# Graph attention on one Trainium2 core: the value product turned, and score rows made on TensorE instead of by DMA

## The chip, the cores and the metric

The kernel runs on one core of one Trainium2 chip. The core has TensorE (PE: matmuls and transposes, with PEld its weight loads), VectorE (DVE), ScalarE (ACT), GpSimd (POOL) and SyncE (SP, which here only issues DMAs). Matmul results land in PSUM, [...]; everything else lives in SBUF or in DRAM. The metric is the device time of one execution in microseconds, less is better. The kernel before takes 3081.6 us, the median of three runs (3081.55 to 3082.2).

## The reference

64 graphs of 256 nodes with 256 features, and an adjacency matrix each. Layer 0 is a normalised, rectified input through three rounds of a gated graph network (message product, sum over neighbours, GRU cell), added to the input. Layer 1 is graph attention with four heads of 64 features, added again:

```python
h = (node_feats @ W.T + b).reshape(Bb, Nn, Hh, Cc)
l_src = jnp.einsum('bihc,hc->bih', h, a_src)
l_dst = jnp.einsum('bjhc,hc->bjh', h, a_dst)
logits = jax.nn.leaky_relu(l_src[:, :, None, :] + l_dst[:, None, :, :], ALPHA)
logits = jnp.where(adj_matrix[..., None] == 1, logits, NEG_INF)
probs = jax.nn.softmax(logits, axis=2)
out = jnp.einsum('bijh,bjhc->bihc', probs, h)
```

For a node i and a head, the score of neighbour j is a number of i plus a number of j; the softmax over j weighs the value vectors h of all j. All of it is f32.

## The kernel before, in words

The graphs are worked on in 32 pairs. A pair is T = 512 nodes: PB = 2 graphs of KN = 2 tiles of 128 nodes, R = 4 tiles r. `pair(p)` is a Python generator that writes out the work of one pair and yields between steps. The loop at the end keeps two pairs alive and takes one step of each in turn: pair p is in the second half of its steps (end of the GRU, then attention) while pair p+1 is in its first half (normalisation, GRU). A pair has 23 yields (`STEPS`), and a new pair starts every `STEPS // 2 + 1` = 12 steps. The order in which steps are written gives each instruction a priority; a planner in the framework then makes one instruction stream per engine, in which work of a later step goes ahead where an earlier one would leave the engine idle by the planner's own costs. On the chip each engine takes its stream in order, and waits on semaphores that the framework places.

PSUM is split in two pools of four banks: `ps_g` for the GRU gates, and `ps_m`, tag `mm`, handed out by `bank(...)`, for every other TensorE result. A bank is free again when its readers are done.

The steps of a pair: normalise and transpose (L242 to L247); three rounds of halves / aggregate / two gate steps (L248 to L303, `gate` at L233); `x1`, the sum with the input (L306); normalise again (L314); `val` (L316), for each tile of nodes 264 columns: 256 value features, then 4 numbers of i and 4 of j, one per head. Then come the steps that the change touches:

- Score rows (L326 to L335). The four j-columns of `val` are transposed into a [4, 512] block `prow` (4 transposes), copied to SBUF as `srow` by ScalarE, written to DRAM (`flat`) and read back onto all 128 partitions as `rows_` by a second DMA, both on SP's queue.
- Scores (L338 to L350), one step per graph: for each tile of 128 nodes i and each head, VectorE adds row, i-number and mask into `zz` [128, 4, 256], then applies the leaky slope in place.
- Softmax (L351 to L374), one step per tile: negated maximum on VectorE, exponentials on ScalarE with their sum `den`, reciprocal `rden`, and 8 transposes (`ppT`), whose copies, one by each of ScalarE and VectorE, make `prT`: probabilities with j on the partitions.
- Value product (L375 to L387), at the start of the next step: for each head and each half of j, `prT` is stationary (128 columns) and 64 value columns are moving; the result `po` has i on the partitions. VectorE multiplies by `rden` into `o`, GpSimd adds `x1`, and after both graphs SP stores `o`.

Of the kernel before, what the change touches and what calls it, by code (L numbers as in the profile page):

```python
# [9 lines left out]
F32 = mybir.dt.float32  # L10
# [3 lines left out]
ALU = mybir.AluOpType  # L14
AX = mybir.AxisListType

P = 128
# [3 lines left out]
ALPHA = 0.2  # L21
# [4 lines left out]
def gated_gnn_then_gat_kernel(  # L26
# [27 lines left out]
    nc = tc.nc  # L54
    B, N, D = x.shape
    L = weight.shape[0]
    H, C2 = a.shape
    C = C2 // 2
    G = 3 * D // P
    KD = D // P  # L60
    KN = N // P
    PB = 2
    R = PB * KN
    T = PB * N
# [3 lines left out]
    ctx.enter_context(nc.allow_non_contiguous_dma(reason="biases and attention vectors, once"))  # L68
    const = ctx.enter_context(tc.tile_pool(name="const", bufs=1))
    io = ctx.enter_context(tc.tile_pool(name="io", bufs=2))  # L70
    dram = ctx.enter_context(tc.tile_pool(name="dram", bufs=2, space=bass.MemoryType.DRAM))
    ps_g = ctx.enter_context(tc.tile_pool(name="ps_g", bufs=4, space=bass.MemoryType.PSUM))
    ps_m = ctx.enter_context(tc.tile_pool(name="ps_m", bufs=4, space=bass.MemoryType.PSUM))

    def bank(name):
        return ps_m.tile([P, 512], F32, tag="mm", name=name)
# [23 lines left out]
    ident = const.tile([P, P], F32, name="ident")  # L100
# [138 lines left out]
    def pair(p):  # L239
# [82 lines left out]
                )  # L322
            nc.vector.tensor_add(val[:, r, :], pt[:, :VW], b_val)
        yield

        pt = bank(f"prow_{p}")  # L326
        for r in range(R):
            nc.tensor.transpose(pt[:H, ts(r, P)], val[:, r, D + H :], ident)
        srow = small.tile([H, T], F32, tag="srow", name=f"srow_{p}", bufs=2)
        nc.scalar.copy(srow, pt[:H, :])  # L330
        flat = dram.tile([H, T], F32, tag="flat", name=f"flat_{p}")
        nc.sync.dma_start(flat, srow)
        rows_ = sb.tile([P, H, T], F32, tag="rows", name=f"rows_{p}")
        nc.sync.dma_start(rows_, bass.AP(tensor=flat.tensor, offset=flat.offset, ap=[[0, P], [T, H], [1, T]]))
        yield  # L335
        o = sb.tile([P, R, D], F32, tag="o", name=f"o_{p}")
        for i in range(PB):
            lks = []  # L338
            for s in range(KN):
                r = i * KN + s  # L340
                zz = sb.tile([P, H, N], F32, tag="zz", name=f"zz_{p}_{r}")
                for h in range(H):
                    nc.vector.scalar_tensor_tensor(  # L343
                        zz[:, h, :], rows_[:, h, ts(i, N)], val[:, r, D + h : D + h + 1],
                        noedge[:, r, :], op0=ALU.add, op1=ALU.add,
                    )
                zf = zz.rearrange("q h n -> q (h n)")
                nc.vector.scalar_tensor_tensor(zf, zf, ALPHA, zf, op0=ALU.mult, op1=ALU.max)
                lks.append(zz)
            yield  # L350
            for s in range(KN):  # L351
                r = i * KN + s
                lk = lks[s]
                nmx = small.tile([P, H], F32, tag="nmx", name=f"nmx_{p}_{r}")
                nc.vector.tensor_reduce(nmx, lk, AX.X, ALU.max, negate=True)  # L355
                den = small.tile([P, H], F32, tag="den", name=f"den_{p}_{r}")
                pr = sb.tile([P, H, N], F32, tag="pr", name=f"pr_{p}_{r}")
                for h in range(H):
                    nc.scalar.activation(  # L359
                        pr[:, h, :], lk[:, h, :], AF.Exp, bias=nmx[:, h : h + 1], accum_out=den[:, h : h + 1]  # L360
                    )
                rden = small.tile([P, H], F32, tag="rden", name=f"rden_{p}_{r}")
                nc.vector.reciprocal(rden, den)
                prT = sb.tile([P, KN, H, P], F32, tag="prT", name=f"prT_{p}_{r}")
                for j in range(KN):
                    pt = bank(f"ppT_{p}_{r}_{j}")
                    for h in range(H):
                        nc.tensor.transpose(pt[:, ts(h, P)], pr[:, h, ts(j, P)], ident)  # L368
                    dst = prT[:, j].rearrange("q h n -> q (h n)")
                    if j % 2:  # L370
                        nc.vector.tensor_copy(dst, pt)
                    else:
                        nc.scalar.copy(dst, pt)  # L373
                yield  # L374
                po = bank(f"po_{p}_{r}")  # L375
                for h in range(H):
                    for j in range(KN):
                        nc.tensor.matmul(  # L378
                            po[:, ts(h, C)], prT[:, j, h, :], val[:, i * KN + j, ts(h, C)],
                            start=(j == 0), stop=(j == KN - 1),  # L380
                        )
                nc.vector.tensor_mul(  # L382
                    o[:, r, :].rearrange("q (h c) -> q h c", h=H),
                    po[:, :D].rearrange("q (h c) -> q h c", h=H),
                    rden[:, :, None].to_broadcast([P, H, C]),
                )
                nc.gpsimd.tensor_add(o[:, r, :], o[:, r, :], x1[:, r, :])  # L387
        nc.sync.dma_start(out_rows[ts(p, T), :].rearrange("(r q) d -> q r d", q=P), o)


    STEPS = 1 + L * (2 + KD) + 4 + PB * (1 + KN)
    live = []
    nxt, tick = 0, 0
    while nxt < NPAIR or live:
# [38 lines left out]
```

## Time and profile before

| | before |
|---|---|
| median of the runs | 3081.6 us |
| the profiled execution, its span | 3082.2 us, 3080.4 us |
| granted TensorE clock, mean | 0.986 |
| TensorE busy (matmul) | 2895.8 us, 94% |
| VectorE, ScalarE, GpSimd busy | 56%, 33%, 18% |
| DMA, mean | 29 GB/s |
| value product `po`, L378 | 2048 instructions |
| probability transposes `ppT`, L368 | 1024 instructions |
| read-back `rows<-flat` | 32 DMAs of 1024 KB |

How to read it: an engine's busy share is an average over the span. Matmuls are pipelined, so the durations of single ones overlap, and their sum overstates the work; the distance between the starts of a long run of the same kind is the cost of one. In a row of groups, the operands are out<-in, then partitions x elements, the count, busy time, mean ns of one, and the idle time of the engine just before them with what ended it.

### The profile page before, as it was taken

To read this page: it belongs to the slowest core of one execution; us is meant where nothing else is said; L and a number is where in the kernel's file an instruction comes from. 1 tells how busy PE (TensorE), PEld (TensorE's weight loads), DVE (VectorE), ACT (ScalarE), POOL (GpSimd) and SP (SyncE) were. 2 spreads that over 40 slices of the span, in tenths; PEclk is the share of its full clock that TensorE was granted. 3 is DMA by queue.
4 is the path that set the end of the run, shared out by engine and by line. 5 is a ranking of instruction groups with operands and counts; after the bars stand their busy time and mean duration, and the time that the engine had idled before them with its cause. 6 is when DMAs were issued, how large, how long until landed. Compare 5 with 4: busy or idle time off the path is not lost.

```text
span 3080.4 us, 30164 instructions
## 1 busy us (share of the span) xinstructions
PE 2895.8 (94%) x11236; PEld 1668.7 (54%) x11236; DVE 1715.3 (56%) x3390; ACT 1021.9 (33%) x2247; POOL 559.0 (18%) x583
## 2 busy tenths in 40 slices
PE   7999999999999999999999999999999999999995
PEld 4455555555555555555555555555555555555554
DVE  3465655555664556554556554656555555645554
ACT  1233333333332333332333333333323333323332
POOL 0121111112112121111211111111111112111111
PEclk9999999999999999999999999999999999999996
DMA  2000000000001001001000100000010010000000
GB/s 84 21 21 28 28 34 29 21 29 33 28 28 35 21 28 35 28 28 35 21 28 29 34 28 33 23 28 28 28 35 21 28 35 28 28 35 8 21 21 21
DMA packets 60947, 88.84 MB, mean 29 GB/s; under 512 B 4736, under 2 KB 56576, under 8 KB 56704
## 3 DMA queue, kind: packets, MB, share of 16 engines
q1 hardware_dynamic: 55552, 84.16, 8.0%
q10 hardware_dynamic: 5248, 2.76, 0.3%
q8 instruction: 88, 1.44, 0.2%
q14 instruction: 59, 0.48, 0.1%
HBM read 69.87 MB, written 17.04 MB: 28 GB/s over the span
## 4 chain that ended last, share of the span: by engine, by line
PE 83%; DVE 9%; ACT 3%; POOL 3%; issue 1%; DMA 1%; SPq 0%; DVEq 0%; POOLq 0%; ACTq 0%
PE pr L235 19%; PE pz L235 19%; PE pin L235 11%; PE phn L235 8%; PE po L378 8%; PE pa L264 7%; PE pv L320 4%; PE ppT L368 3%; ACT pr L359 2%; PE pn L228 2%; POOL d L299 1%; DVE x L310 1%; DVE st_b L199 1%; DVE zz L343 1%; DVE nmx L355 1%
## 5 line engine op out<-in xcount | busy, mean ns | idle before, releaser
L289 POOL TENSOR_SCALAR z<-z 128x512 f32<-128x512 f32 x192 | 140.5, 732 | 1310.9 <-ACT z L288 1310.9
L235 PE MATMUL pr<-aggr,w_in 128*128 128x512 f32 x768 | 361.0, 592 | 0.0
L235 PE MATMUL pz<-aggr,w_in 128*128 128x512 f32 x768 | 360.9, 592 | 0.0
L235 PE MATMUL pin<-aggr,w_in 128*128 128x512 f32 x768 | 360.9, 592 | 0.0
L285 ACT ACTIVATE r<-pr,brz 128x512 f32<-128x512 f32 x192 | 131.9, 687 | 688.6 <-PE pr L235 688.6
L294 DVE TENSOR_TENSOR t<-pin,t 128x512 f32<-128x512 f32 x192 | 132.5, 690 | 359.6 <-PE pin L235 358.5
L300 DVE TENSOR_TENSOR d<-z,d 128x512 f32<-128x512 f32 x192 | 132.9, 692 | 328.9 <-POOL d L299 327.9
L359 ACT ACTIVATE pr<-zz,nmx 128x256 f32<-128x256 f32 x512 | 254.3, 500 | 105.6 <-DVE nmx L355 105.6
L378 PEld LDWEIGHTS po<-val,prT 128*128 128x128 f32 x2048 | 253.1, 196 | 41.2 <-issue 14.8
L288 ACT ACTIVATE z<-pz,brz 128x512 f32<-128x512 f32 x192 | 131.3, 684 | 397.0 <-PE pz L235 397.0
L286 DVE TENSOR_SCALAR r<-r 128x512 f32<-128x512 f32 x192 | 81.6, 425 | 323.0 <-ACT r L285 323.0
L378 PE MATMUL po<-val,prT 128*128 128x64 f32 x2048 | 256.5, 277 | 2.4 <-ACT prT L373 1.6
L235 PE MATMUL phn<-hT,hh_T 128*128 128x512 f32 x512 | 254.8, 599 | 0.0
L235 PE MATMUL pr<-hT,hh_T 128*128 128x512 f32 x512 | 252.8, 596 | 0.0
L235 PE MATMUL pz<-hT,hh_T 128*128 128x512 f32 x512 | 246.0, 592 | 0.0
L235 PEld LDWEIGHTS pin<-aggr,w_in 128*128 128x128 f32 x768 | 145.9, 190 | 183.7 <-issue 183.7
L235 PEld LDWEIGHTS pz<-aggr,w_in 128*128 128x128 f32 x768 | 145.9, 190 | 183.7 <-issue 183.7
L235 PEld LDWEIGHTS pr<-aggr,w_in 128*128 128x128 f32 x768 | 143.5, 190 | 156.0 <-issue 146.1
L387 POOL TENSOR_TENSOR o<-o,x 128x256 f32<-128x256 f32 x128 | 107.0, 836 | 648.8 <-DVE o L382 609.2
L343 DVE SCALAR_TENSOR_TENSOR zz<-rows,val,noedge 128x256 f32<-128x256 f32 x512 | 214.8, 476 | 7.2 <-DMA rows<-flat 7.2
L368 PE MATMUL ppT<-ident,pr 128*128 128x128 f32 x1024 | 164.5, 285 | 49.8 <-ACT pr L359 44.8
L299 POOL TENSOR_TENSOR d<-hT,n 128x512 f32<-128x512 f32 x128 | 161.6, 1263 | 188.0 <-ACT n L296 188.0
(96 smaller groups left out, 4343.2 us busy)
## 6 DMA issues: line engine op xcount, KB each, us to landing
rows<-flat SPq DMA_DIRECT2D x32, 1024.0 KB
x<-in_x_dram SPq DMA_DIRECT2D x32, 512.0 KB
adj<-in_adj_dram SPq DMA_DIRECT2D x32, 512.0 KB
out_dram<-o SPq DMA_DIRECT2D x32, 512.0 KB
w_msg<-in_L_gnn_weight_dram ACTq DMA_DIRECT2D x1, 768.0 KB
ih_nat<-in_L_gnn_w_ih_dram ACTq DMA_DIRECT2D x1, 768.0 KB
hh_nat<-in_L_gnn_w_hh_dram ACTq DMA_DIRECT2D x1, 768.0 KB
flat<-srow SPq DMA_DIRECT2D x32, 8.0 KB
```

What stands on the lines that cost most here:

```text
L235: nc.tensor.matmul(pt, w[:, k, ts(g, P)], src[:, k, :], start=start and k == 0, stop=stop and k == KD - 1)
L264: nc.tensor.matmul(pt[:, ts(i, N)], y[:, r, ts(e, P)], edge[:, r, :], start=(j == 0), stop=(j == len(parts) - 1),)
L285: nc.scalar.activation(r_, p_r, AF.Tanh, bias=brz[:, g_r : g_r + 1], scale=0.5)
L288: nc.scalar.activation(z_, p_z, AF.Tanh, bias=brz[:, g_z : g_z + 1], scale=0.5)
L289: nc.gpsimd.tensor_scalar(z_, z_, 0.5, 0.5, op0=ALU.mult, op1=ALU.add)
L294: nc.vector.tensor_add(t_, p_in, t_)
L299: nc.gpsimd.tensor_sub(d_, hT[:, c, :], n__)
L300: nc.vector.tensor_mul(d_, z_, d_)
L343: nc.vector.scalar_tensor_tensor(zz[:, h, :], rows_[:, h, ts(i, N)], val[:, r, D + h : D + h + 1], noedge[:, r, :], op0=ALU.add, op1=ALU.add,)
L359: nc.scalar.activation(pr[:, h, :], lk[:, h, :], AF.Exp, bias=nmx[:, h : h + 1], accum_out=den[:, h : h + 1])
L368: nc.tensor.transpose(pt[:, ts(h, P)], pr[:, h, ts(j, P)], ident)
L378: nc.tensor.matmul(po[:, ts(h, C)], prT[:, j, h, :], val[:, i * KN + j, ts(h, C)], start=(j == 0), stop=(j == KN - 1),)
```

## The change

Two parts of attention are replaced, and the steps are cut differently.

The score rows no longer go through DRAM. For each graph, head and half of j, TensorE transposes one column of `val`, broadcast to 128 columns, so that every partition of the result holds the row: 8 transposes per graph into two banks `rowp`, each with two heads. VectorE reads them from PSUM, and the leaky slope now writes a second tile `lk`.

The value product is turned. `prT` collects both tiles of a graph, so that a head's probabilities are [128 of j, 256 of i] and are moving, and the 64 value columns of the head are stationary. The result has features on the partitions: head 2 h2 on 0 to 63 and head 2 h2 + 1 on 64 to 127 of one bank `po`. ScalarE copies it to `oT`, four transposes per graph turn it back into a bank `pob`, and one multiply and one add per graph (512 columns, not 256) finish it. The product now waits for both tiles of the graph, and the transposes back stand one step later.

`STEPS` becomes 24: the step for the rows is gone, and each graph has one more for the turning back. The interval between pairs becomes 13.

```diff
-        pt = bank(f"prow_{p}")
-        for r in range(R):
-            nc.tensor.transpose(pt[:H, ts(r, P)], val[:, r, D + H :], ident)
-        srow = small.tile([H, T], F32, tag="srow", name=f"srow_{p}", bufs=2)
-        nc.scalar.copy(srow, pt[:H, :])
-        flat = dram.tile([H, T], F32, tag="flat", name=f"flat_{p}")
-        nc.sync.dma_start(flat, srow)
-        rows_ = sb.tile([P, H, T], F32, tag="rows", name=f"rows_{p}")
-        nc.sync.dma_start(rows_, bass.AP(tensor=flat.tensor, offset=flat.offset, ap=[[0, P], [T, H], [1, T]]))
-        yield
         o = sb.tile([P, R, D], F32, tag="o", name=f"o_{p}")
         for i in range(PB):
+            rowp = []
+            for h2 in range(H // 2):
+                pt = bank(f"prow_{p}_{i}_{h2}")
+                for hh in range(2):
+                    col = D + H + 2 * h2 + hh
+                    for s in range(KN):
+                        nc.tensor.transpose(
+                            pt[:, hh * N + s * P : hh * N + (s + 1) * P],
+                            val[:, i * KN + s, col : col + 1].to_broadcast([P, P]),
+                            ident,
+                        )
+                rowp.append(pt)
...
                     nc.vector.scalar_tensor_tensor(
-                        zz[:, h, :], rows_[:, h, ts(i, N)], val[:, r, D + h : D + h + 1],
+                        zz[:, h, :], rowp[h // 2][:, ts(h % 2, N)], val[:, r, D + h : D + h + 1],
                         noedge[:, r, :], op0=ALU.add, op1=ALU.add,
                     )
-                zf = zz.rearrange("q h n -> q (h n)")
-                nc.vector.scalar_tensor_tensor(zf, zf, ALPHA, zf, op0=ALU.mult, op1=ALU.max)
-                lks.append(zz)
+                lk = sb.tile([P, H, N], F32, tag="lk", name=f"lk_{p}_{r}")
+                zf, lf = (y.rearrange("q h n -> q (h n)") for y in (zz, lk))
+                nc.vector.scalar_tensor_tensor(lf, zf, ALPHA, zf, op0=ALU.mult, op1=ALU.max)
+                lks.append(lk)
             yield
+            prT = sb.tile([P, KN, H, N], F32, tag="prT", name=f"prT_{p}_{i}")
+            rden = small.tile([P, KN, H], F32, tag="rden", name=f"rden_{p}_{i}")
...
-                    dst = prT[:, j].rearrange("q h n -> q (h n)")
+                    dst = prT[:, j, :, ts(s, P)]
+                    src = pt.rearrange("q (h n) -> q h n", h=H)
...
                 yield
-                po = bank(f"po_{p}_{r}")
-                for h in range(H):
-                    for j in range(KN):
+            po = bank(f"po_{p}_{i}")
+            for h2 in range(H // 2):
+                for j in range(KN):
+                    for hh in range(2):
+                        h = 2 * h2 + hh
                         nc.tensor.matmul(
-                            po[:, ts(h, C)], prT[:, j, h, :], val[:, i * KN + j, ts(h, C)],
+                            po[hh * C : (hh + 1) * C, ts(h2, N)], val[:, i * KN + j, ts(h, C)], prT[:, j, h, :],
                             start=(j == 0), stop=(j == KN - 1),
                         )
-                nc.vector.tensor_mul(
-                    o[:, r, :].rearrange("q (h c) -> q h c", h=H),
-                    po[:, :D].rearrange("q (h c) -> q h c", h=H),
-                    rden[:, :, None].to_broadcast([P, H, C]),
-                )
-                nc.gpsimd.tensor_add(o[:, r, :], o[:, r, :], x1[:, r, :])
+            oT = sb.tile([P, H // 2, N], F32, tag="oT", name=f"oT_{p}_{i}")
+            nc.scalar.copy(oT.rearrange("q h n -> q (h n)"), po)
+            yield
+            pb_ = bank(f"pob_{p}_{i}")
+            for s in range(KN):
+                for h2 in range(H // 2):
+                    nc.tensor.transpose(pb_[:, s * D + h2 * P : s * D + (h2 + 1) * P], oT[:, h2, ts(s, P)], ident)
+            rows = slice(i * KN, (i + 1) * KN)
+            nc.vector.tensor_mul(
+                o[:, rows, :].rearrange("q r (h c) -> q (r h) c", h=H),
+                pb_.rearrange("q (x c) -> q x c", c=C),
+                rden.rearrange("q s h -> q (s h)")[:, :, None].to_broadcast([P, KN * H, C]),
+            )
+            of, xf = (y[:, rows, :].rearrange("q r d -> q (r d)") for y in (o, x1))
+            nc.gpsimd.tensor_add(of, of, xf)
...
-    STEPS = 1 + L * (2 + KD) + 4 + PB * (1 + KN)
+    STEPS = 1 + L * (2 + KD) + 3 + PB * (2 + KN)
```

More of the change, by code (lines that the diff above doesn't have):

```diff
@@ L70, in gated_gnn_then_gat_kernel @@
     io = ctx.enter_context(tc.tile_pool(name="io", bufs=2))
-    dram = ctx.enter_context(tc.tile_pool(name="dram", bufs=2, space=bass.MemoryType.DRAM))
     ps_g = ctx.enter_context(tc.tile_pool(name="ps_g", bufs=4, space=bass.MemoryType.PSUM))
@@ L361, in pair @@
                     )
-                rden = small.tile([P, H], F32, tag="rden", name=f"rden_{p}_{r}")
-                nc.vector.reciprocal(rden, den)
-                prT = sb.tile([P, KN, H, P], F32, tag="prT", name=f"prT_{p}_{r}")
+                nc.vector.reciprocal(rden[:, s, :], den)
                 for j in range(KN):
@@ L368, in pair @@
                         nc.tensor.transpose(pt[:, ts(h, P)], pr[:, h, ts(j, P)], ident)
-                    dst = prT[:, j].rearrange("q h n -> q (h n)")
+                    dst = prT[:, j, :, ts(s, P)]
+                    src = pt.rearrange("q (h n) -> q h n", h=H)
                     if j % 2:
-                        nc.vector.tensor_copy(dst, pt)
+                        nc.vector.tensor_copy(dst, src)
                     else:
-                        nc.scalar.copy(dst, pt)
+                        nc.scalar.copy(dst, src)
```

## The prediction

> **What bounds the kernel now.** I read the page first: busy time by engine and the chain that ended last.
>
> ```profile
> span 3080.4 us, 30164 instructions
> PE 2895.8 (94%) x11236; PEld 1668.7 (54%) x11236; DVE 1715.3 (56%) x3390; ACT 1021.9 (33%) x2247; POOL 559.0 (18%) x583
> ...
> PE 83%; DVE 9%; ACT 3%; POOL 3%; issue 1%; DMA 1%; SPq 0%; DVEq 0%; POOLq 0%; ACTq 0%
> ```
>
> TensorE is busy 94% of the span and holds 83% of the chain; no other engine passes 56%. Work taken off or put on TensorE should therefore move the end, and work on the others should not, unless TensorE comes to wait for it. The waits of TensorE itself are the second view (total us, times, longest):
>
> ```profile
> PE pt_b L219 <- DVE xn_b L206: 78.7, 32, 4.4
> PE ppT L368 <- ACT pr L359: 44.8, 33, 13.1
> PE pn_b L228 <- DVE hT L301: 24.1, 32, 4.2
> ```
>
> Each comes about once per pair. None is for the score rows. The only wait for those is VectorE's, in the groups:
>
> ```profile
> L343 DVE SCALAR_TENSOR_TENSOR zz<-rows,val,noedge 128x256 f32<-128x256 f32 x512 | 214.8, 476 | 7.2 <-DMA rows<-flat 7.2
> ```
>
> It is 7.2 us in all, in the last pair. The transfer is hidden everywhere else.
>
> Busy durations of matmuls overlap, so I price TensorE from the third view, the timeline, by start to start:
>
> ```profile
> 1295.76 1.89 PE L378 MATMUL po<-val,prT 128*128 128x64 f32 x16
> 1297.49 1.94 PE L235 MATMUL phn<-hT,hh_T 128*128 128x512 f32 x4
> 1299.26 1.88 PE L235 MATMUL pr<-hT,hh_T 128*128 128x512 f32 x4
> 1300.98 1.88 PE L235 MATMUL pr<-aggr,w_in 128*128 128x512 f32 x4
> ...
> 1307.84 1.04 PE L368 MATMUL ppT<-ident,pr 128*128 128x128 f32 x8
> 1308.72 0.38 PE L228 MATMUL pn<-ident,hT 128*128 128x128 f32 x2
> 1309.12 0.43 PE L378 MATMUL po<-val,prT 128*128 128x64 f32 x2
> ...
> 1350.43 3.73 PE L320 MATMUL pv<-w_val,hT_b 128*128 128x264 f32 x16
> 1353.99 1.88 PE L235 MATMUL pr<-aggr,w_in 128*128 128x512 f32 x4
> ```
>
> One `po` instruction takes (1297.49 - 1295.76)/16 = 0.108 us, a gate instruction of 512 columns 1.72/4 = 0.43, a transpose 0.88/8 = 0.11, a 264-column one 3.56/16 = 0.2225. An f32 product is two instructions (the 1024 products of L378 are 2048), a transpose one. `po` moves 64 columns, an eighth of a gate's, yet costs a quarter of a gate's time: it pays for loading 128 weight columns, not for streaming. The same place of the pattern (`po` x2) starts at 1309.12 and again at 1401.92, so a pair takes 92.8 us. TensorE's own work per pair: gates 144 x 0.43 = 61.9; `pa` 48 x 0.119 = 5.7 (16 instructions take 1.9); the transposes `pn`, `pt`, `prow`, `ppT` 76 x 0.11 = 8.4; `pv` 3.6; `po` 64 x 0.108 = 6.9. That is 86.5, which leaves 6.3 us per pair of waits and ramps.
>
> [...] a gate matmul lasts 592 ns, 0.43 of which is its turn, so its tail is about 0.16 us. [...]
>
> **The change, part by part**, per pair of graphs unless said.
>
> *Score rows.* Removed: 4 `prow` transposes (0.44), one ScalarE copy (575 ns), two DMAs on SP's queue. Added: 16 transposes of one column broadcast to 128, at 0.11 as the other 128x128 ones: 1.76. Net +1.32 on TensorE. A broadcast operand is not in the trace; loading 4 columns (`prow`) and 128 columns both gave 0.11, because the streamed identity sets the pace, so below 0.11 I see nothing and the upper bound is the 0.19 of an f32 weight load (+1.3); I take 0.11. SP loses waits for `srow` and issues x, adj and out no later; VectorE waited only 10.6 us for x in the whole span, so that is worth nothing. VectorE's zz now reads PSUM. From L343 (476 ns, 256 elements) and L348 (1218, 1024) a 512-element one is 723 ns in SBUF, and L291 from PSUM takes 750: 27 ns x 512 = 14 us of VectorE in the span, hidden by its 44% of idle time.
>
> *The product.* Removed: 64 `po` instructions, 6.91. Added: 8 products per graph, 16 instructions of 256 columns. A turn is 0.43/2 = 0.215 (0.2225 x 256/264 = 0.216 agrees). In order of issue each head's two instructions follow each other, then the other head's two: the second of one head can run beside the first of the other. So 16 instructions make 9 turns, 1.94 us a graph, 3.87 a pair. Entirely serial it is 6.88.
>
> *Turning back.* 8 transposes: 0.88. ScalarE gains a 512-column copy (586 ns, x64, less `srow`: +19 us in the span), VectorE does 64 multiplies of 690 instead of 128 of 423, GpSimd 64 adds of 1263 instead of 128 of 836: all off the path. The transposes wait for that copy, and gates queue behind them on TensorE; but they stand a step later, behind the other pair's `pa` or gates, which cover 0.6 us. Uncovered it would be 0.59 + 0.16 = 0.75 a graph.
>
> *Mode switches.* In before one `po` block in four is split by a gate (the x2 at 1309.12). I take 2.5 blocks per pair, 5 switches x 0.163 = 0.82. Lower bound 0; upper, with the next weight load exposed too, 5 x (0.163 + 0.19) = 1.77.
>
> *Steps.* 23 becomes 24 and a new pair starts every 13 steps, not 12: the last gate step of the third round has no partner step. Neighbouring work is planned ahead across steps (the next pair's `st_a` runs at 1532), so nothing on TensorE is lost. The zz step moves from beside `halves` to beside gates (10.3 us), which may end the 0.94 us wait of `ppT`; in exchange the later product has less to put into the wait for `hT`. I count them as even.
>
> *Banks.* Two of the four `mm` banks are held while VectorE does zz, 8 x 0.42 (214.8 us of L343 over 512) + 1.22 = 4.6 us at least. Gates, which run beside it, use the other pool, so I cost it at nothing; without this cover it is up to 4.6 x 64 us.
>
> Sum: 3.87 + 1.76 + 0.88 + 0.82 - 7.35 = -0.02 a pair, **-1 us** over 32 pairs.
>
> *The end.* The last pair's attention runs alone. There zz starts at 3041.97, when the rows land, while the first two tiles of `val` stand at 3033.0 and `pv` ends at about 3034. Eight cold transposes (0.22) put the start near 3036: -6. Two `po` blocks of 3.7 become one of 9 x 0.43 = 3.9 per graph, -3; copy, transposes and the longer multiply and add cost +2 to +3 at the very end. **-7 us**.
>
> So 3082.2 (the profiled execution; its span is 3080.4, 1.8 around it) - 8 = 3074.2; the median of the runs is 0.6 lower: **3074**.
>
> **The rivals.**
>
> *A, heads side by side (the forecast), 60%.* Its own range: without switch costs -0.84 x 32 = -27, and -10 at the end: 3045; with the dear switches +0.93 x 32 = +30, -7: 3104.
>
> *B, the two heads run one after the other, 30%; this is the one on the other side.* Place: the product; 6.88 in place of 3.87 and no gain over the 6.91 removed, so all 16 + 8 - 4 transposes are net cost: +2.17 x 32 = +69, less 5 at the end: **3146**, between 3116 (the `ppT` wait of 30 us filled) and 3172 (switches too). For it: no trace shows f32 column tiles, and each pass reloads weights. [...] It decides from 7.35 - 2.64 = 4.71 us a pair: a factor of 6.88/4.71 = 1.46 between the heads breaks even, 1.77 with the five switches.
>
> *C, side by side, but a wait takes the place, 10%.* TensorE stands at the transposes back until the ScalarE copy is done, or at a `mm` bank: 64 x 0.75 = 48 us: **3122**. For it: in-order issue, four banks. Against: ScalarE is busy 33%.
>
> *The row transfer was on the path and its removal is the gain.* Only 7.2 us of waiting speaks for it; that is inside the -7.
>
> **How the numbers follow.** A repeat of this kernel can tell 0.2% (6 us). A: faster in 0.55 of it, same 0.2, slower 0.25; B and C are slower. Faster 0.33, same 0.12, slower 0.55. A is likeliest, hence 3074, with its own range 3045 to 3104. The whole range goes up into B, to 3155: left out are about a tenth of A and the upper third of B, under 2 in 10.
>
> **What would show it.** Right: two products of different heads start within some ns of each other, 16 of them in about 2 us, then a gap near 0.16 before the next kind; the DMA share falls; the waits of TensorE keep their three lines. Wrong: 16 products in 3.4 us (B); a new line of TensorE waiting for `oT` or for zz (C); broadcast transposes over 0.11 apart; gaps over 0.3 at each switch.

## The result, and the profile after

The changed kernel takes 3149.9 us, the median of four runs (3145.84 to 3150.82), against 3081.68 us of the kernel before in the same series: a ratio of 1.0219, with a 95% interval from 1.0201 to 1.0236. It is 68 us slower. The forecast was 3074 us. The profiled execution took 3145.84 us with a span of 3144.0, where before it was 3082.2 and 3080.4.

The page of the kernel after: its span, the busy time by engine, and the chain that ended last.

```profile
span 3144.0 us, 29237 instructions
...
PE 2948.7 (94%) x10852; PEld 1599.2 (51%) x10852; DVE 1708.7 (54%) x3326; ACT 1031.8 (33%) x2279; POOL 538.9 (17%) x519
...
PE 77%; DVE 9%; POOL 6%; issue 4%; ACT 3%; DMA 1%; SPq 0%; DVEq 0%; POOLq 0%; ACTq 0%
```

TensorE issues 384 instructions fewer and shows 53 us more of busy time. Its share of the chain falls from 83% to 77%, and what gains is GpSimd (3 to 6%) and issue (1 to 4%). The waits of TensorE after (total us, times, longest):

```profile
PE pt_b L218 <- DVE xn_b L205: 78.6, 32, 4.3
PE pn L227 <- DVE hT L300: 25.1, 64, 1.7
PE pv L319 <- ACT hT_b L219: 18.2, 32, 0.6
PE ppT L371 <- ACT pr L364: 12.8, 6, 6.0
```

Against before, the wait of `ppT` fell from 44.8 to 12.8 us; two came in its place. One is `pn` for hT, which stood so among the waits before:

```profile
PE pn L228 <- DVE hT L301: 3.3, 2, 1.7
```

The other is `pv` for `hT_b` (0.5 us, once, before). Together these waits changed by 32 us down and 40 up, so waits alone don't explain 68 us. The groups of the kernel after that answer to the score rows and the product, by line (busy us, mean ns of one, then idle time before and what ended it):

```profile
L385 PE MATMUL po<-prT,val 128*64 128x256 f32 x1024 | 180.7, 401 | 2.4 <-ACT prT L377 0.9
L319 PE MATMUL pv<-w_val,hT_b 128*128 128x264 f32 x512 | 172.1, 506 | 18.2 <-ACT hT_b L219 18.2
L395 PE MATMUL pob<-ident,oT 128*128 128x128 f32 x256 | 38.4, 272 | 1.4 <-ACT oT L390 1.4
L344 DVE SCALAR_TENSOR_TENSOR zz<-prow,val,noedge 128x256 f32<-128x256 f32 x512 | 211.8, 476 | 59.4 <-PE prow L333 59.4
```

The surprise is the second row. The value projection `pv`, which the change does not touch, is 506 ns an instruction now. Before, its row was:

```profile
L320 PE MATMUL pv<-w_val,hT_b 128*128 128x264 f32 x512 | 123.2, 395 | 0.5 <-ACT hT_b L220 0.5
```

The last row of the groups after shows VectorE waiting 59.4 us for the rows, where it waited 7.2 us for the DMA before.

Two stretches of the timeline (start us, duration, then the instructions) show where TensorE's time goes. First the end of a GRU round of one pair beside the value product of the other:

```profile
1308.34 0.38 PE L227 MATMUL pn<-ident,hT 128*128 128x128 f32 x2
1308.74 0.65 PE L385 MATMUL po<-prT,val 128*64 128x256 f32 x4
1309.32 1.13 PE L234 MATMUL phn<-hT,hh_T 128*128 128x512 f32 x2
1310.38 1.51 PE L385 MATMUL po<-prT,val 128*64 128x256 f32 x10
1312.58 0.87 PE L227 MATMUL pn<-ident,hT 128*128 128x128 f32 x6 [0.69 <-DVE hT L300]
1313.38 0.65 PE L385 MATMUL po<-prT,val 128*64 128x256 f32 x2
1313.96 1.12 PE L234 MATMUL phn<-hT,hh_T 128*128 128x512 f32 x2
```

The heads do run side by side: four `po` instructions take 1309.32 - 1308.74 = 0.58 us, which is two turns of 0.215 and 0.15 more. But the product of every graph is cut in three pieces (4, 10, 2), so there are 12 changes into or out of it in a pair, not 5. The second stretch is the second normalisation:

```profile
1377.09 1.31 PE L218 MATMUL pt_b<-ident,xn_b 128*128 128x128 f32 x8 [2.41 <-DVE xn_b L205]
1378.98 5.27 PE L319 MATMUL pv<-w_val,hT_b 128*128 128x264 f32 x16 [0.58 <-ACT hT_b L219]
1383.89 0.48 PE L263 MATMUL pa<-edge,hi_a 128*128 128x256 f32 x1
```

Before, the other pair's first-round products `pa` (16 of them, the sum over neighbours in its first round) stood between and behind the `pt_b`:

```profile
1347.61 0.41 PE L219 MATMUL pt_b<-ident,xn_b 128*128 128x128 f32 x2 [2.41 <-DVE xn_b L206]
1347.78 0.37 PE L264 MATMUL pa<-edge,hi_a 128*128 128x256 f32 x1
```

There `pv` took 1353.99 - 1350.43 = 3.56 us. Now `pa` stands behind `pv`, which takes 1383.89 - 1378.98 = 4.91 us. The same microseconds in 1-us windows (length, then busy time and count of PE, PEld, DVE, ACT and POOL, then the granted TensorE clock, DMA share and GB/s):

```profile
1378.00:1379.00 1.00, 0.42 (x4) 0.18 (x3) 0.66 (x3) 0.67 (x2) 0.19 (x1) 0.76 0.00 0
1379.00:1380.00 1.00, 1.00 (x2) 0.81 (x3) 0.14 (x1) 0.41 (x1) 0.82 (x1) 0.50 0.00 0
1380.00:1381.00 1.00, 1.00 (x4) 0.77 (x3) 1.00 (x4) 0.00 (x0) 0.00 (x0) 0.50 0.00 0
1381.00:1382.00 1.00, 1.00 (x4) 0.79 (x3) 0.24 (x1) 0.00 (x0) 0.00 (x0) 0.53 0.00 0
1382.00:1383.00 1.00, 1.00 (x6) 0.84 (x6) 0.86 (x2) 0.00 (x0) 0.00 (x0) 1.00 0.00 0
```

The granted clock is at one half for about 3.4 us, while `pv` runs; below, this is called a dip. It comes in all ten pairs that lie between 1000 and 2000 us here, and in three of ten or eleven in the kernel before. What it costs is seen in the kernel before, whose pairs take 92.8 us without a dip and 94.3 with one: 1.5 us. In the traces of before, of after and of twelve of the runs below, the dips between 1000 and 2000 us begin whole multiples of 3.413 us apart within each trace; each lasts one such length, or two in some of the runs. What sets that length is not shown. TensorE did not stand idle all the time ahead of this dip (2.41 us of standing, eight transposes, 0.58 us of standing): what went ahead was a thin stretch, one in which TensorE has little to do. In the 3.41 us ahead of this dip (1375.11 to 1378.52) TensorE was busy for 1.31 us; so it was, within 0.03 us, ahead of all ten. Ahead of the three dips of the kernel before it was busy for 1.0 to 1.1 us; of its other stretches of 3.41 us between 1000 and 2000 us, counted in step with the dips, the thinnest had 1.5, and no dip followed it.

### Where a pair's time goes

A turn is the distance from the start of one instruction to the start of the next in a row of the same kind. For the pairs between 1000 and 2000 us I price each instruction by its turn (0.108 us for a `po`, 0.11 a transpose, and so on) and put whatever remains up to the next start to the two kinds it lies between. The rows are good to about 0.1 us; the last two columns have the same instructions, and their work differs by 0.07. In us per pair:

| | before | after | `pa` one step earlier (below) |
|---|---|---|---|
| work at the price of its turns | 86.84 | 85.50 | 85.57 |
| ahead of `pt_b` | 2.58 | 2.57 | 2.57 |
| around `pv` | 0.23 | 2.49 | 0.32 |
| around `po` | 0.30 | 3.66 | 3.65 |
| around `ppT` | 2.04 | 0.00 | 0.00 |
| everything else | 1.34 | 1.35 | 1.32 |
| a pair | 93.33 | 95.57 | 93.43 |

The work fell, by some 1.3 us. The pair grew by 2.24, which over the 31 steps from one pair to the next is +69; the end behind the last `val` fell from 45.6 to 39.3 us, -6. That is +63, beside +64 between the two profiled executions and +68 between the medians.

### The profile page after: what moved, and what is told of

Same layout as the page of the kernel before. It is cut to its first block, busy times and chain, and to the rows that moved or that the text cites. A ratio compares the mean times of both kernels' runs of the same rounds, so it can differ in the third digit from the quotient of the medians.

```text
span 3144.0 us, 29237 instructions
## 1 busy us (share of the span) xinstructions
PE 2948.7 (94%) x10852; PEld 1599.2 (51%) x10852; DVE 1708.7 (54%) x3326; ACT 1031.8 (33%) x2279; POOL 538.9 (17%) x519
## 4 chain that ended last, share of the span: by engine, by line
PE 77%; DVE 9%; POOL 6%; issue 4%; ACT 3%; DMA 1%; SPq 0%; DVEq 0%; POOLq 0%; ACTq 0%
PE pz L234 19%; PE pr L234 19%; PE pin L234 9%; PE phn L234 7%; PE pa L263 6%; PE pv L319 5%; POOL d L298 4%; PE ppT L371 2%; DVE d L299 2%; DVE hT L300 2%; PE pn L227 2%; PE prow L333 2%; ACT n L295 2%; DVE x L309 1%; PE pt_b L218 1%
## 5 line engine op out<-in xcount | busy, mean ns | idle before, releaser
L288 POOL TENSOR_SCALAR z<-z 128x512 f32<-128x512 f32 x192 | 149.0, 776 | 1340.0 <-ACT z L287 1340.0
L364 ACT ACTIVATE pr<-lk,nmx 128x256 f32<-128x256 f32 x512 | 253.7, 498 | 134.0 <-DVE nmx L360 133.7
L234 PE MATMUL phn<-hT,hh_T 128*128 128x512 f32 x512 | 269.1, 618 | 0.0
L344 DVE SCALAR_TENSOR_TENSOR zz<-prow,val,noedge 128x256 f32<-128x256 f32 x512 | 211.8, 476 | 59.4 <-PE prow L333 59.4
L267 ACT COPY aggr<-pa 128x512 f32<-128x512 f32 x192 | 112.6, 586 | 332.8 <-PE pa L263 332.8
L371 PEld LDWEIGHTS ppT<-ident,pr 128*128 128x128 f32 x1024 | 126.4, 142 | 131.7 <-issue 71.4
L319 PE MATMUL pv<-w_val,hT_b 128*128 128x264 f32 x512 | 172.1, 506 | 18.2 <-ACT hT_b L219 18.2
L385 PE MATMUL po<-prT,val 128*64 128x256 f32 x1024 | 180.7, 401 | 2.4 <-ACT prT L377 0.9
```

The costliest lines, as they stand in the source:

```text
L234: nc.tensor.matmul(pt, w[:, k, ts(g, P)], src[:, k, :], start=start and k == 0, stop=stop and k == KD - 1)
L288: nc.gpsimd.tensor_scalar(z_, z_, 0.5, 0.5, op0=ALU.mult, op1=ALU.add)
L319: nc.tensor.matmul(pt[:, :VW], hT[:, k, ts(r, P)], w_val[:, k, :], start=(k == 0), stop=(k == KD - 1))
L344: nc.vector.scalar_tensor_tensor(zz[:, h, :], rowp[h // 2][:, ts(h % 2, N)], val[:, r, D + h : D + h + 1], noedge[:, r, :], op0=ALU.add, o ...
L364: nc.scalar.activation(pr[:, h, :], lk[:, h, :], AF.Exp, bias=nmx[:, h : h + 1], accum_out=den[:, h : h + 1])
L385: nc.tensor.matmul(po[hh * C : (hh + 1) * C, ts(h2, N)], val[:, i * KN + j, ts(h, C)], prT[:, j, h, :], start=(j == 0), stop=(j == KN - 1),)
```

## The experiments

The theories: **O**, the new interval moved work of the two pairs against each other, and TensorE lost the cover it had (at `pv`), that is, the work that filled its waits; **S**, the product's cuts and mode switches are the loss (a mode switch is a change on TensorE between the product's instructions, `128*64` in the rows above, and the `128*128` ones); **R**, the score rows on TensorE are the loss; and the prediction's rivals, the heads one after the other (B) and a wait for the `oT` copy or a bank (C). C is refuted by the trace after: `pob` waited 1.4 us for `oT` in the whole span, and no TensorE wait there is for a bank.

**The two heads in turn.** Only the order of issue changes.

```diff
-                for j in range(KN):
-                    for hh in range(2):
+                for hh in range(2):
+                    for j in range(KN):
```

> The changed kernel with each head's four product instructions issued in one row (head outside, half of j inside), so that only the instructions at a change of head can run beside each other: 13 turns a graph instead of 9. If the two column tiles do run side by side: 4 x 0.215 x 64 = +55 us, 3205, less what falls into waits (3175 to 3205). If they never did: 3150 within 10 us.

Measured: 3185.26 us, a ratio of 1.0335 [1.032, 1.035]; 35 us over the changed kernel. In the timeline of this run the pieces have become 2, 10 and 4:

```profile
1229.04 1.51 PE L385 MATMUL po<-prT,val 128*64 128x256 f32 x10
1230.90 0.88 PE L227 MATMUL pn<-ident,hT 128*128 128x128 f32 x6 [0.36 <-DVE hT L300]
1231.71 1.08 PE L385 MATMUL po<-prT,val 128*64 128x256 f32 x4
```

The last four, now of one head, take 1.00 us where four of two heads took 0.58: two turns more. Two turns of 0.215 in 64 graphs are 27.5 us of the 35; the rest may be dips, four of eleven of which are of double length in this run; that was not shown. So the heads overlap where both are at hand, and B falls: that its 3146 lies near the result is chance.

**The interval, in both kernels.** The changed kernel with a new pair every 12 steps, and the kernel before with 13:

```diff
-        if nxt < NPAIR and tick % (STEPS // 2 + 1) == 0:
+        if nxt < NPAIR and tick % (STEPS // 2) == 0:      # changed kernel: 12
+        if nxt < NPAIR and tick % (STEPS // 2 + 2) == 0:  # kernel before: 13
```

> The changed kernel with a new pair every 12 steps, as before the change, and nothing else. Theory O (order: with 13 steps between pairs the next pair's aggregation stands behind pv instead of ahead of it, TensorE idles 0.6 us more there, its clock drops to 0.70 and pv takes 4.9 us instead of 3.6; about 1.9 us a pair): 3150 - 61 = 3089, less what else the order saves, 3050 to 3090; mean clock back to 0.98 or more; pv mean near 395 ns. Theory S (the product itself: mode switches and the added transposes are the loss): 3130 to 3150.

> The kernel before the change with a new pair every 13 steps instead of 12, and nothing else. Theory O: 3082 + 61 = about 3143, pv mean near 500 ns, clock near 0.976. Theory S: 3082 within 10 us.

Measured: the kernel before at 13 takes 3197.76 us, 1.0381 [1.0364, 1.0398]. The interval alone costs it 116 us, more than the whole change does. In it `pv` is at 517 ns, and dips, some of double length, come in every pair or nearly so. For O, that settles the sign. At the same 13 steps, then, the changed kernel is 48 us faster than the kernel before: of the +68, the interval by itself is worth +116 in the old kernel, and the rest of the change -48. The changed kernel at 12, however, takes 3146.03 us, 1.0204 [1.0189, 1.0219]: no gain, a miss for O, in the range of S. There `pv` is back at 389 ns, and the product is whole:

```profile
1311.68 1.95 PE L385 MATMUL po<-prT,val 128*64 128x256 f32 x16
1313.56 1.13 PE L234 MATMUL pr<-hT,hh_T 128*128 128x512 f32 x2
```

Sixteen instructions take 1.88 us, 8 turns and 0.16. Both things that look wrong in the changed kernel are mended, and the time is the same, because `pn` now waits 67.3 us for hT (25.1) and `ppT` 31.0 for `pr` (12.8) and 21.5 for `prT`, the copy that frees its bank. A mended stretch tells nothing while another stretch moves with it. What was needed were runs that move one thing.

**Filling the stretch ahead of `pv`.** Eight more transposes of `xn` between `pt_b` and `pv`; nothing uses what they compute.

```diff
+        fill = bank(f"fill_{p}")
+        for r in range(R):
+            for k in range(KD):
+                nc.tensor.transpose(fill[:, ts(r, P)], xn[:, r, ts(k, P)], ident)
```

> The changed kernel with eight more transposes per pair, useless ones, of which four (0.44 us) stand between pt_b and pv, where TensorE waits 0.58 us for the hT_b copies; all else as in the changed kernel. Theory O with the clock as its larger part: the wait is filled, the clock stays up, pv falls from 4.9 to 3.6 us: 3150 - 32 x 1.3 = 3108, up to 3130 if it helps in part. If the slow pv is not the clock's doing: 3150 to 3165.

Measured: 3138.21 us, 1.018 [1.0165, 1.0195]: 12 us less than the changed kernel, with 28 us of work added (256 x 0.11), and between the two ranges. `pv` takes 3.43 us in the pair at 1377 us and 428 ns an instruction over the run (506 in the changed kernel, 395 before). But the dip has not gone: it comes in nearly every pair still. For part of the run it lies a little earlier, on `pt_b` and the added transposes; from pair to pair it moves on until it lies on `pv` again. What was gained is the standing ahead of `pv`, and that part of the half clock falls on work that is worth nothing.

**`pa` one step earlier, the interval still 13.** The one experiment that puts back the order and nothing else; no step is added.

```diff
-            yield
+            if l:
+                yield
             aggr = sb.tile([P, KD, T], F32, tag="aggr", name=f"aggr_{n_}")
...
             yield
+            if not l:
+                yield
             hT2 = sb.tile([P, KD, T], F32, tag="hT", name=f"hT_{n_}", bufs=4)
```

> The changed kernel at its 13-step interval, with the first-round products pa of a pair written one step earlier, so that they stand between the transposes pt_b and the product pv of the pair ahead again, as they do in the kernel before; nothing else is changed. Order theory (the 13-step interval put pa behind pv, so TensorE stands before pt_b, runs down its granted clock and has no cover left for the halves): the pv stretch goes back from 4.9 to about 3.6 us and pv from 506 to about 395 ns, 61 to 80 us in all, 3070 to 3090. Switch theory (the loss is mostly the cuts of the product, 12 mode switches in a pair): the cuts stay, 3120 to 3150.

Measured: 3081.25 us, 0.9996 [0.9987, 1.0005]. All of the loss is gone, 69 us. The timeline of this run where the changed kernel stood:

```profile
1348.27 0.41 PE L218 MATMUL pt_b<-ident,xn_b 128*128 128x128 f32 x2 [2.41 <-DVE xn_b L205]
1348.43 0.37 PE L264 MATMUL pa<-edge,hi_a 128*128 128x256 f32 x1
...
1352.17 4.19 PE L322 MATMUL pv<-w_val,hT_b 128*128 128x264 f32 x16
```

`pa` fills in between the `pt_b`, and `pv` no longer waits for `hT_b` (0.5 us in the span, 18.2 before the edit). The last column of the table above is this run: only the row around `pv` moves, from 2.49 to 0.32. Dips now come in four of ten or eleven pairs, and those pairs take 94.4 us, the others 92.9; the pair shown has one, and its `pv` took 4.03 us. So of the 2.14 us that the edit saves in a pair, 0.6 fewer dips at 1.5 us are about 0.9, and the rest, about 1.2, is the standing ahead of `pv` and the slower row of `pt_b` alone (an estimate from the table). The row around `po` did not move at all. So the order, by itself, is enough to undo the loss, and S is not needed for it. What S explains is that this run is no faster than before: by the table, 3.35 us more around `po` stand against 1.27 us of work saved and 2.04 us of waits around `ppT` gone. That is a balance of accounts, not shown by a run: none took all the cuts away alone at 13 steps. Nor is it shown what ended the wait of `ppT`; the interval alone did not, for `ppT` still waits 40.8 us for `pr` in the kernel before at 13 steps, and 39.9 us in the changed kernel with its rows by DMA.

**Is it the stretch or its phase?** The 95.57 us of a pair are 28.0 times the 3.413 us that space the dips, so the dip might merely have fallen in step with the pairs. I added transposes elsewhere, behind `pob`, to change the period (4, 8 and 12 per pair):

```diff
+            if i == PB - 1:
+                fill = bank(f"fill_{p}")
+                for k in range(4):
+                    nc.tensor.transpose(fill[:, ts(k % 4, P)], oT[:, k % 2, ts(k // 2 % 2, P)], ident)
```

> The changed kernel with 4 more transposes in each pair, written behind the transposes back (pob) of its second graph; nothing uses what they compute. By their own time they add 4 x 0.11 x 32 = 14 us. In the records of the changed kernel a stretch of half granted clock, about 3.4 us long and 1.5 us dear, comes in every pair at pv; in the kernel before it comes in every third. Thin-stretch theory: the stretch before pv is thin in every pair whatever its phase, so the dip still comes in every pair and the time is 3164. Phase theory: [...] 95.57 us a pair is just 28.0 of them, which keeps the dip in step with the pairs; another period loosens it, the dip comes in some pairs only, and the time is 3150 or less although work is added.

> As the run with 4 more transposes, with 8 of them: 28 us of their own time. Thin-stretch theory: 3178. Phase theory: dips in part of the pairs, 3130 to 3165.

> As the run with 4 more transposes, with 12 of them: 42 us of their own time. Thin-stretch theory: 3192. Phase theory: dips in part of the pairs, 3150 to 3178.

Measured: 3161.87, 3184.6 and 3196.75 us, or 12, 35 and 47 us over the changed kernel, for 14, 28 and 42 us of added work. As it was put, the phase theory falls: at each of these periods most pairs have a dip (8, 11 and 10 begin between 1000 and 2000 us), and a third to a half of the dips are of double length. So they came with the thin stretch at all four periods. But phase still counts where the stretch is less thin: the kernel before stands 2.41 us ahead of `pt_b` in every pair, and one pair in three is hit. Its dips begin at 1161.55, 1441.44 and 1721.34 us, three pairs or 82.0 times 3.413 us apart.

**The product alone, the rows alone.** First the changed kernel with the rows by DMA again (the block of `prow`, `srow`, `flat` and `rows_`, the read-back in one buffer, in the step of the scores; 13 steps). Then the kernel before with rows on TensorE, where the old block becomes an empty step (23 steps, interval 12):

```diff
-                        zz[:, h, :], rowp[h // 2][:, ts(h % 2, N)], val[:, r, D + h : D + h + 1],
+                        zz[:, h, :], rows_[:, h, ts(i, N)], val[:, r, D + h : D + h + 1],
```

> The changed kernel with the score rows by DMA again (the read-back has one buffer and the leaky slope works in place, for room), interval 13. If the transposes for the rows cost their work: 3150 - 42 = 3108. If they stand in waiting time: 3150 within 10 us. Either way the waits for hT and the slow pv stay, by theory O.

> The kernel before the change with the score rows made by broadcast transposes on TensorE, as in the changed one, and the product, the steps (the rows' step is kept, empty) and the interval of 12 as before. If rows cost their work: 12 more transposes of 0.11 us a pair, 1.32 x 32 = +42: 3124. If they fall into waits of TensorE: under 3100. If the two banks they hold or the moved scores cost cover as well: over 3140.

Measured: 3117.77 us, 1.0117 [1.0102, 1.0132] for the first, 32 us under the changed kernel, near the 42 that 1.32 x 32 gives for the added transposes; between its two forecasts, nearer the first. The second takes 3353.57 us, 1.0885 [1.0869, 1.0901], of which the 12 added transposes of a pair explain 42 of 272 us over before. Its waits of TensorE name the place of more:

```profile
PE ppT L371 <- ACT pr L362: 114.5, 33, 5.8
```

It was 44.8, so that is 70 us. And TensorE dips twice in nearly every pair, once for double the time. A dip of 3.4 us at one half takes away 1.7 us of full clock, and cost 1.5 us in the kernel before. In 1000 us the dips here take away 47.8 us of full clock, where they took 5.1 before; at that cost, and over some 3.1 such stretches, I estimate the difference at about 115 us. The remaining 45 us are not explained. R has a second price, then, as I read it: VectorE waited 7.2 us in all for rows that came by DMA (before) and 59.4 us for rows made on TensorE (after); those come when TensorE's stream gets to them, and everything behind them, scores, exponentials and `ppT`, follows late. The runs with the rows one step earlier, below, test this.

**Shorter intervals.** The two kernels at 11 steps:

```diff
-        if nxt < NPAIR and tick % (STEPS // 2 + 1) == 0:
+        if nxt < NPAIR and tick % (STEPS // 2 - 1) == 0:  # changed kernel
+        if nxt < NPAIR and tick % (STEPS // 2) == 0:      # kernel before
```

> The changed kernel with a new pair every 11 steps. The next pair's aggregation and gates then stand beside the second normalisation, so that gates fill the 2.6 us that TensorE waits ahead of pt_b, and pv runs at full clock. Theory O: 2.57 x 32 = -82 and 1.9 x 32 = -61 against 3150, up to 60 of it given back where the wait for hT has less to cover it: 3005 to 3070. Theory S (the product and its switches are the loss, whatever the order): 3130 or more.

> The kernel before the change with a new pair every 11 steps instead of 12. Theory O: the 2.57 us wait ahead of pt_b is filled: 3082 - 82 = 3000, up to 60 given back: 3000 to 3060. Compared with the changed kernel at 11, the two products stand under like cover: by work alone the changed one has 1.3 us a pair less, less its switches, so 20 to 40 us less time. Theory S: 3082, and the changed kernel at 11 is 60 or more slower than this.

Measured: the kernel before gains, 3026.22 us, 0.9822 [0.9806, 0.9839], without a dip between 1000 and 2000 us. The changed kernel loses, 3357.28 us, 1.0897 [1.0881, 1.0913]; I had expected the opposite. Its timeline and its waits:

```profile
1315.10 1.04 PE L333 MATMUL prow<-ident,val 128*128 128x128 f32 x8
...
1327.37 1.91 PE L371 MATMUL ppT<-ident,pr 128*128 128x128 f32 x8 [3.40 <-ACT pr L364]
```

```profile
PE ppT L371 <- ACT pr L364: 222.1, 68, 6.0
```

From the rows of a graph to its first `ppT` it is 12.3 us here, in which VectorE and ScalarE make the probabilities; at this interval TensorE gets there first and stands, and dips twice a pair.

**Rows written one step earlier**, at 11 and at 12 steps; the eight transposes of the first graph go to the end of the `val` step, those of the second behind the `oT` copy of the first.

```diff
-            rowp = []
+        def score_rows(i):
+            rowps[i] = []
...
+        score_rows(0)
         yield
...
             nc.scalar.copy(oT.rearrange("q h n -> q (h n)"), po)
+            if i + 1 < PB:
+                score_rows(i + 1)
             yield
```

> The changed kernel at an interval of 11 with its row transposes written one step earlier (beside gates of the other pair, at the end of the value step and of the first product's step), nothing else. If the 3357 us of the changed kernel at 11 come from scores that can only start once TensorE reaches the rows, with too little work between them and ppT: the 7 us a pair ahead of ppT fall to 2 or less, 3357 - 160 = 3195 or less. If they come from the two banks held, or from the interval itself: 3357, or more.

> The changed kernel at a 12-step interval, with the transposes that spread the score rows written one step earlier than in the first run at 12 steps. If the late start of the rows holds the scores and so the probabilities at 12 steps, the waits ahead of ppT (about 1.9 us in a pair) go: near 3086. If the loss at 12 steps is elsewhere (hT of the halves), no change from 3146.

Measured: 3052.57 us at 11, 0.9904 [0.9889, 0.9918], 305 us less than with the rows in their place; 3053.34 us at 12, 0.9908 [0.9893, 0.9922], 93 less than the first run at 12, more than the 60 expected. The wait of `ppT` for `pr` is 13.3 us in both (222.1 and 31.0). So the start of the rows was the loss at these intervals. At 12 fewer pairs dip too, two of ten or eleven where it was six. Against the kernel before at 11 steps (3026.22 us) both are still behind.

**Fewer cuts at 13 steps.** The product takes the second half of j first.

```diff
-                for j in range(KN):
+                for j in reversed(range(KN)):
...
-                            start=(j == 0), stop=(j == KN - 1),
+                            start=(j == KN - 1), stop=(j == 0),
```

> The changed kernel, interval 13, with the two halves of j in reverse order in the product, so that its first instruction needs the copy that comes last and the block is cut in two pieces instead of three. If a cut costs two mode switches of 0.2 us: two cuts a pair less, 32 x 2 x 0.4 = -26: 3124. If the switches cost nothing, or the wait for hT grows by as much: 3150 within 6 us.

Measured: 3150.76 us, 1.0222 [1.0207, 1.0237], the same. The pieces are 14 and 2, two per graph, but `pn` waits 52.7 us for hT where it waited 25.1. One piece is gone, and its two switches had stood in a time that TensorE now spends waiting for hT: at this place they were free.

**The turned product with rows by DMA, in a step of their own** (25 steps), at 12 and 11. The rows' block and its `yield` are those of the kernel before, with `rows_` in one buffer; the product is the changed one.

```diff
+        rows_ = sb.tile([P, H, T], F32, tag="rows", name=f"rows_{p}", bufs=1)
+        nc.sync.dma_start(rows_, bass.AP(tensor=flat.tensor, offset=flat.offset, ap=[[0, P], [T, H], [1, T]]))
+        yield
...
-        if nxt < NPAIR and tick % (STEPS // 2 + 1) == 0:
+        if nxt < NPAIR and tick % 11 == 0:
```

> The same with a new pair every 12 steps. The product alone, at the interval of the kernel before: by work -2.6 + switches 0.5 = -2.1 us a pair, 3082 - 67 = 3015, if its cover is as in before; about 3080 to 3110 if the product, now for two tiles at once, leaves the wait for hT uncovered as it did in the changed kernel at 12 (1.4 to 2.3 us a pair).

> The turned product with the score rows by DMA in a step of their own (25 steps; read-back in one buffer, leaky slope in place), a new pair every 11 steps. If the loss of the change is cover lost on TensorE and not the product: work 84.2 us a pair as in the run with DMA rows at 13, and at most the waits of the kernel before at 11 (4.8 us) plus 0.5 to 1 of mode switches: 89.5 to 90 us a pair, 2960 to 2990, below both kernels. If the switches or the later product eat the gain: 3026 (the kernel before at 11) or more.

Measured: 3098.28 us at 12, 1.0052 [1.0036, 1.0069]; 2974.59 us at 11, 0.965 [0.9636, 0.9665]. The first is in the upper range of its forecast, with the wait for hT at 58.3 us; the latter is faster than both kernels. Between 1000 and 2000 us it has no dip. Against the kernel before at the same interval it is 51.6 us quicker: 1.33 us a pair over 32 pairs (91.47 to 90.14) are 43 of it. The lines of its page:

```profile
span 2972.5 us, 28717 instructions
...
PE 2799.3 (94%) x10468; PEld 1506.8 (51%) x10468; DVE 1713.0 (58%) x3326; ACT 1043.6 (35%) x2311; POOL 534.7 (18%) x519
```

Its TensorE is busy for 94% of the span, as in the kernel before (3081.68 us) and in the changed one (3149.9 us): that share tells nothing of which is the good one.

**All intervals side by side.** Medians in us; the edits are those named above.

| steps between pairs | kernel before | changed kernel | changed, rows one step earlier | turned product, rows by DMA |
|---|---|---|---|---|
| 11 | 3026.22 | 3357.28 | 3052.57 | 2974.59 |
| 12 | 3081.68 | 3146.03 | 3053.34 | 3098.28 |
| 13 | 3197.76 | 3149.9 | not run | 3117.77 (rows in the step of the scores) |

Beside the kernel before at the same interval, the changed kernel is 331 us slower at 11 steps, 64 slower at 12 and 48 faster at 13. The turned product with rows by DMA is 52 faster, 17 slower and 80 faster.

## Why the prediction was right or wrong

- **The likeliest case named the right mechanism and the wrong time.** The kernel before has no column tiles; that two heads would overlap, with one bank `po` between them, was my estimate, and the runs show it: the heads run side by side, so the swap works in f32 too. For what the prediction says of `po` before, that it paid for its weight loads, the trace has this: PEld is busy for all of the 1.73 us (1295.76 to 1297.49) of the 16 instructions priced there. The price of the product was even too high, since 16 instructions make 8 turns, not 9, when they are not cut (1.88 us less 0.16).
- **The step that failed is "Steps"**: 23 to 24 steps and the interval of 13, of which it said that "nothing on TensorE is lost". It costs 2.26 us a pair around `pv`, 72 us in all; writing `pa` a step earlier took 69 us back. The evidence given was one `st_a` ahead of its step; it showed that planning across steps occurs, not that it would put `pa` back in this place. The waits that the prediction shows begin with `pt_b`, 32 times; what stands between that wait and `pv` in the timeline before is `pa` of the other pair, the very work that one step of shift moves.
- **In "Steps" too, "I count them as even" was off, to the good.** The wait ahead of `ppT` went as foreseen (2.04 us a pair around it, where 0.94 was named), and the wait for hT came as foreseen, but only 0.68 us of it (3.3 to 25.1 us in the span). That the shift of the scores ended the first is not shown.
- **"Mode switches" was mis-sized.** 5 switches at 0.163 us, 0.82; that a switch costs a pause was my estimate, sized by the tail of a gate matmul. There are 12; those with no wait in them cost 0.14 to 0.20 us by the starts of the rows shown, and the cuts part some heads from their partners, so that a graph takes 10 turns for 8. Product and switches were to be 4.69 us a pair; the work row's 3.46 and the 3.66 around `po`, less 0.78 of waiting for hT, are 6.34. The count was taken from how the planner had cut the product before; a cut that cost 0.05 to 0.06 us there (from `po` to a gate and back) costs about 0.35 here (0.15 and 0.20 in the first stretch shown). Not all of that need be the mode: from `pn` to `po`, both `128*128` there, the kernel before lost 0.18 us too (1308.72 to 1309.12, less two transposes).
- **"Score rows" held for TensorE** (16 x 0.11, broadcast or not) and left out the start of the rows, which the changed kernel's waits do not show at 13 steps and which rules at 12 and 11. VectorE's `zz` from PSUM is 476 ns, as from SBUF; the 27 ns added for it are not there, and with VectorE idle for 46% of the span they need not have shown.
- **"Turning back" and "Banks" held**: 0.88 us, 1.4 us of waiting for `oT`, and no wait for a bank among TensorE's. "The end" was forecast at -7 and is -6.
- **The rivals.** The time fell into the range through something none of them was. B's 3146 is 4 us away and its mechanism is refuted; C's waits are not there. The missing rival was the plain one: the interval as such, with nothing else changed, which costs 116 us in the kernel before.

In one sum: -0.02 forecast; +2.26 around `pv`, +1.65 for product and switches over their price, +0.78 of waiting for hT, -2.04 around `ppT`, and some -0.4 of small terms (the 0.30 around `po` before is the largest) make the 2.24 that was measured.

## What to carry to other kernels

When a change adds or drops a step of interleaved work, list for each stretch where the bounding engine is thin what the other stream has there, and shift that list by the new offset before you call the schedule even; here one step was worth 69 us in the changed kernel, and all the work that the change saves on TensorE about 40 (1.27 x 32). Compare two designs at the same interval and each at its best one: with rows by DMA the turned product gains 52 us at 11 steps and loses 17 at 12, and the change as it was made costs 64 us at 12 and gains 48 at 13. A result moved from a DMA queue to the bounding engine's stream is bound to its place there, so ask what then starts late: the row transposes written one step earlier took 305 us off at 11 steps.

## What the runs showed that I had not expected

- A thin stretch of 4.3 us (2.41 us standing, eight transposes, 0.58 us standing) was followed by a granted clock of 0.50 for about 3.4 us, at 1.5 us a time (the price in the kernel before), in every pair; 2.41 us of standing with denser work behind it was followed by that in one pair of three (the kernel before) or in four of ten or eleven (the run with `pa` earlier). The mean clock hardly shows it: 0.986 before, 0.976 after. The 1-us windows do.
- Column tiles in f32: pairs of heads start every 0.215 us, the turn of one head alone. Two instructions of one head first and then two of the other still overlap within a block of ten (the run of the heads in turn: 1.51 us of work for 10 in both orders), so in this block the issue order between tiles need not alternate one by one.
- A stationary operand of one column broadcast to 128 costs a transpose the same 0.11 us (eight row transposes in 0.88 us, 1315.10 to 1315.98, in the changed kernel at 11 steps).
